# A mixture-of-experts stage: nested branches, fixed sets of blocks, other chunk sizes

## The chip, the cores and the metric

The kernel runs on one core of a Trainium2 chip. The metric is the device time of one launch in microseconds, lower is better. The engines are named as in the profile: PE (TensorE: matmuls; PEld is its weight load), DVE (VectorE), ACT (ScalarE), POOL (GpSimd) and SP (SyncE, here only a queue for DMAs).

## The reference, cut to what matters

Two layers on x of shape 32 x 128 x 56 x 56 in fp32. The first is a depthwise 7x7 convolution, a LayerNorm over the channels and a mixture of 8 experts; the second is a coordinate attention with a 3x3 convolution.

```python
T = N * H * W                                  # 100352 tokens of C = 128
logits = xf @ Wg + bg
topv, topi = jax.lax.top_k(logits, 2)          # two experts for each token
wts = softmax(topv)
order = argsort(-wts[:, 0])                    # the surest tokens first
cap = int(1.25 * T / 8)                        # 15680 places for each expert
# a token beyond its expert's places gets nothing from that expert
h = gelu(eb @ W1[e] + b1[e])                   # 128 -> 512
y = h @ W2[e] + b2[e]                          # 512 -> 128
moe[token] = sum over its experts of gate * y
x = input + x_skip + layer_scale * moe
# second layer
x_h, x_w = means of x over rows and columns    # (and over their first halves and quarters)
a_h, a_w = sigmoid(...), sigmoid(...)
out = conv3x3(x * a_w * a_h); out = out * sigmoid(out)   # with a batch norm between
```

How many tokens an expert gets depends on the data. Here experts 0, 3, 6 and 7 are full (15680), experts 1, 2, 4 and 5 get 7551, 12576, 578 and 1713.

## The kernel before

The stages follow one another: the depthwise convolution (L144, to about 600 us of the profile), LayerNorm, logits and top-2 (L227, to about 1327), the experts (to 3316), and the coordinate attention (L894 to L987, to the end). After the second of these a row for each token lies in DRAM, `acc_d`: its 128 channels, 8 gates and a number of the expert, RW = 137 floats. The change touches only the stage of the experts.

*Blocks and chunks.* An expert's 15680 places are ST = 123 tiles of 128 rows, 4 tiles make a block, so a full expert has 31 blocks. `CHUNKS` cuts the 31 blocks into five chunks. A block passes these steps:

- `gather` (L591): four indirect DMAs, issued by POOL, read 4 x 128 rows of `acc_d` by the list of indices `idx` into a tile `xg`.
- `turn` (L602, L604): PE transposes the four tiles to `pt`, DVE copies them to `fxt`.
- `front` (L612, L613): PE multiplies by W1 into `ph`, ACT applies the gelu and writes `ht`.
- `back` (L621 to L641): PE multiplies by W2 into `py`; DVE computes `own` and the rows to write (`row`, L632, L633), ACT copies the block to `yo` (L636), DVE adds bias, gate and sum (L639 to L641).
- `scatter` (L646): four indirect DMAs, issued by POOL, write the rows of `yo` back to `acc_d` at `row`.

`compute(e, c, ...)` does the middle three for all blocks of a chunk c of expert e, whether they hold tokens or not. `gathers(e, c)` and `scatters(e, c)` are Switches on POOL alone, by the number of blocks that the chunk really holds (`taken_blocks`); a block of a begun chunk without tokens is filled by a memset on POOL (L709) instead of a gather. I write g(e,c) and s(e,c) for these two below.

*Branches.* Around the compute of chunks 1 to 4 stands an If on all engines, `taken > CHUNKS[c] * 512` (L769). The four Ifs of an expert stand behind each other. The next gathers, g(e,c+1), are inside the If; the scatters of the chunk before, s(e,c-1), ahead of it. When the If is not taken, its Else runs only the routing steps that were to be interleaved with the compute.

*Routing.* `Routing` finds by bisection and prefix sums which tokens each expert gets, in small DVE and PE steps. The steps of expert 0 run ahead of the loop; those of the later experts are dealt out over the chunks of the earlier ones (`PIECES`).

*Tiles.* `xg` is a ring of 20 blocks, `yo` and `row` are rings of FO = 16. A block whose slot is in use waits for the reader of the slot. `load_weights` (SP's queue) for expert e+1 stands behind chunk 0 of expert e, `weights` (a multiply of W2 by the layer scale on POOL, L666, and small PE and DVE steps) behind its chunk 1.

*Order.* POOL runs in program order: g(e,1), then for e > 0 the first gathers of the next expert g(e+1,0) (for e = 0 only behind its last chunk), then for each chunk s(e,c-1), If, g(e,c+1), with s(e-1,4) of the expert before at chunk 0. The scheduler that lowers the program moved some of it: for experts 0 to 2 the gathers g(e+1,1) and g(e+2,0) are issued ahead of s(e,3). After the loop a memset on all 16 `yo` slots (the fence) gates the DMAs of the next stage.

## Time and profile before

| | us |
|---|---|
| median of 3 runs | 4523.59 (4507.34 to 4524.99) |
| profiled execution, its own time | 4519.41 |
| its span | 4517.7 |
| stage of the experts in it (1327 to 3316) | 1989 |
| PE, DVE, ACT, POOL busy in that stage | 1502, 984, 698, 1404 |
| granted TensorE clock, whole span | 0.888 |

In the profile's rows "A 4.2 [10.04 <-B]" means that the engine was idle for 10.04 us ahead of the instruction and that B is what the records put as the last thing to release it; "issue" stands for no wait that is seen. Branches, semaphore instructions and the issue of DMAs by a queue do not count as busy, so a stretch of control flow looks like an idle engine. Where both are written, the two numbers of a group's row after the count are the busy time in us and the mean of one in ns.

### The profile page before, as it was taken

The numbers are of one execution on the slowest core, as the hardware profiler recorded it, in microseconds if no ns is written. First come the engines' busy times: TensorE is split into PE (matmuls) and PEld (weight loads), VectorE is DVE, ScalarE is ACT, GpSimd is POOL, SyncE is SP. The second block draws the span as 40 slices with busy tenths as digits, with TensorE's granted clock in tenths as the row PEclk, the third lists the DMA queues.
The fourth block names the chain that finished last, engine by engine and source line by source line (L and its number), as shares of the span: only waits on it lengthen the run. The fifth ranks groups of instructions, "written<-read, shape, count | busy, mean of one in ns | idle before, by whom it ended". The sixth has DMA issues, their size and how long they took to land. (4 is left out here: it accounts for less than half of the span.)

```text
span 4517.7 us, 59987 instructions
## 1 busy us (share of the span) xinstructions
PE 3625.3 (80%) x21360; PEld 2369.6 (52%) x21360; DVE 2569.1 (57%) x5914; ACT 1411.3 (31%) x3132; POOL 2550.8 (56%) x1983
## 2 busy tenths in 40 slices
PE   9999998676328896788788446697958999999899
PEld 4555448676316665565565334464634544455444
DVE  1111115888866966886743112232358888888786
ACT  1111115555203432334243222343412333333232
POOL 1000102232217777668677437777769787877775
PEclk9999998787658898798898778898979999999999
DMA  9999995545362121111111111111155555555552
GB/s 172 217 230 216 230 192 195 231 183 236 150 230 56 49 59 51 44 44 46 52 52 56 46 34 52 56 56 56 56 164 187 174 191 194 168 190 171 176 161 77
DMA packets 814971, 587.33 MB, mean 130 GB/s; under 512 B 545984, under 2 KB 751312, under 8 KB 802128
## 3 DMA queue, kind: packets, MB, share of 16 engines
q1 hardware_dynamic: 508816, 328.72, 25.3%
q10 hardware_dynamic: 262336, 157.84, 12.4%
q0 software_dynamic: 43264, 94.64, 7.3%
q8 instruction: 193, 3.16, 0.3%
q14 instruction: 362, 2.97, 0.2%
HBM read 320.96 MB, written 260.09 MB: 129 GB/s over the span
## 5 line engine op out<-in xcount | busy, mean ns | idle before, releaser
L591 POOL DMA_INDIRECT xg<-acc_d,idx x676 | 673.1, 996 | 408.7 <-issue 172.5
L646 POOL DMA_INDIRECT acc_d<-yo,row x676 | 717.1, 1061 | 234.8 <-issue 82.8
L612 PE MATMUL ph<-fxt,w 128*128 128x512 f32 (+1 forms) x1440 | 700.8, 631 | 53.7 <-ACT ht L613 53.7
L613 ACT ACTIVATE ht<-ph,bias 128x512 f32<-128x512 f32 (+1 forms) x720 | 489.5, 682 | 703.7 <-PE ph L612 702.6
L977 PE MATMUL pc<-v,wk 128*128 128x392 f32 x1920 | 706.1, 510 | 0.4 <-POOL v L962 0.4
L621 PEld LDWEIGHTS py<-w,ht 128*128 128x128 f32 x5728 | 664.9, 192 | 64.8 <-issue 58.2
L621 PE MATMUL py<-w,ht 128*128 128x128 f32 x5728 | 670.5, 276 | 0.0
L144 PE MATMUL acc<-xt,band 56*64 56x424 f32 (+3 forms) x7168 | 666.5, 528 | 2.7 <-POOL band L132 2.7
L144 PEld LDWEIGHTS acc<-xt,band 56*64 56x64 f32 x7168 | 337.6, 133 | 331.0 <-issue 273.3
L977 PEld LDWEIGHTS pc<-v,wk 128*128 128x128 f32 x1920 | 349.2, 192 | 308.6 <-issue 105.7
L227 PE MATMUL lnps<-proj,lnyt 128*128 128x136 f32 x1568 | 354.7, 400 | 138.8 <-ACT sq L232 71.8
L612 PEld LDWEIGHTS ph<-fxt,w 128*128 128x128 f32 x1440 | 279.5, 206 | 329.0 <-issue 243.1
L636 ACT ACTIVATE yo<-xg,own 128x137 f32<-128x137 f32 x716 | 238.0, 401 | 634.9 <-DVE own L632 369.6
L227 PEld LDWEIGHTS lnps<-proj,lnyt 128*128 128x128 f32 x1568 | 349.4, 319 | 144.6 <-ACT sq L232 74.5
L157 DVE TENSOR_SCALAR yt<-acc,dwb 128x448 f32<-128x448 f32 x128 | 87.5, 684 | 582.2 <-PE acc L144 425.2
L639 DVE TENSOR_TENSOR ys<-py,b 128x512 f32<-128x512 f32 (+2 forms) x184 | 123.8, 675 | 490.8 <-PE py L621 480.8
L602 PE MATMUL pt<-ident,xg 128*128 128x128 f32 x716 | 137.0, 311 | 329.7 <-issue 159.2
L132 POOL COPY band<-hk 56x392 f32<-56x392 f32 x128 | 65.2, 510 | 572.4 <-issue 502.0
L987 DVE SCALAR_TENSOR_TENSOR y<-pc,y 128x392 f32<-128x392 f32 x640 | 317.6, 554 | 17.7 <-PE pc L977 17.6
L957 POOL TENSOR_TENSOR d<-pad 128x3248 f32<-128x3248 f32 x32 | 228.1, 7127 | 171.2 <-DVE pad L949 171.2
L894 POOL TENSOR_TENSOR cxn<-cxn,cx 128x896 f32<-128x896 f32 x112 | 261.5, 2344 | 68.3 <-DMA cxn<-acc_d 24.5
L602 PEld LDWEIGHTS pt<-ident,xg 128*128 128x128 f32 x716 | 96.3, 161 | 357.9 <-issue 311.2
(225 smaller groups left out, 4653.8 us busy)
## 6 DMA issues: line engine op xcount, KB each, us to landing
xt<-in_x SPq DMA_DIRECT2D x128, 392.0 KB
y_d<-yt ACTq DMA_DIRECT2D x256, 196.0 KB
lnyt<-y_d SPq DMA_DIRECT2D x16, 3136.0 KB
x<-in_x SPq DMA_DIRECT2D x16, 3136.0 KB
cxn<-acc_d SPq DMA_DIRECT2D x112, 448.0 KB
cx<-acc_d SPq DMA_DIRECT2D x112, 448.0 KB
out<-y ACTq DMA_DIRECT2D x64, 784.0 KB
acc_d<-xn SPq DMA_DIRECT2D x16, 1712.5 KB
```

The source lines that it names most:

```text
L144: nc.tensor.matmul(acc[c][half * G : (half + 1) * G, :, lo:hi], lhsT=band[rows, dw, :], rhs=xt[rows, im, lo + s : hi + s], start=(n == 0), ...
L227: nc.tensor.matmul(ps[:, j, :], lhsT=yf[:, self.j0 + g + j, :], rhs=proj, start=True, stop=True)
L591: d = nc.gpsimd.indirect_dma_start(out=xg[0:n, k, :], out_offset=None, in_=acc_d[0:T1, :], in_offset=bass.IndirectOffsetOnAxis(ap=idx[0][0 ...
L602: nc.tensor.transpose(pt[:, k * P : k * P + n], xg[0:n, k, 0:C], ident[0:n, 0:n])
L612: nc.tensor.matmul(ph[:, 0:N_], lhsT=w[0][:, f * P : (f + 1) * P], rhs=xt[:, 0:N_], start=True, stop=True)
L613: nc.scalar.activation(ht[:, f, 0:N_], ph[:, 0:N_], AF.Gelu, bias=w[2][:, f : f + 1])
L621: nc.tensor.matmul(py[0:n, k, :], lhsT=ht[:, f, k * P : k * P + n], rhs=w2[:, f, :], start=(f == 0), stop=(f == NF - 1))
L636: nc.scalar.activation(yo[0:n, k, :], xg[0:n, k, :], AF.Copy, scale=own[0:n, k : k + 1])
L646: d = nc.gpsimd.indirect_dma_start(out=acc_d[:, :], out_offset=bass.IndirectOffsetOnAxis(ap=row[0:n, k : k + 1], axis=0), in_=yo[0:n, k, : ...
L894: nc.gpsimd.tensor_tensor(xn, xn, x2, ALU.add)
L977: nc.tensor.matmul(m[k], lhsT=wk[k][:, dw, :], rhs=v[:, k, rows, dw : dw + W], start=(dw == 0), stop=(dw == 2))
L987: nc.vector.scalar_tensor_tensor(r[x], m[k], f, r[y_], ALU.mult, ALU.add)
```

## The change

The chunks become 4, 7, 7, 7 and 6 blocks (they were 4, 8, 8, 8 and 3). The Ifs of an expert are nested: `chunk(e, c)` calls `chunk(e, c + 1)` inside its own If, so the first one not taken leaves all later chunks, with their Switches, at once; its Else runs all routing steps that are left. The ring of `xg` becomes two sets of 4 blocks for chunk 0, by turns of the expert, and two sets of 7 for the others, by turns of the chunk. `yo` and `row` become two sets of 7, by turns of `e * 5 + c`. The weights of the next expert are loaded and multiplied directly behind compute(e, 0). The first gathers of expert 1 stand behind the whole nest of expert 0.

```diff
@@ -30,9 +30,9 @@
 BLK = 4
 
 
-CHUNKS = (0, 4, 12, 20, 28, -(-ST // BLK))
+CHUNKS = (0, 4, 11, 18, 25, -(-ST // BLK))
 NC_ = len(CHUNKS) - 1
-CB = 8
+CB = 7
 RW = C + E + 1
 T1 = T + P
 ZF = 16
@@ -554,13 +554,12 @@
                 return out
 
 
-        FO = 16
         cp1 = st.enter_context(tc.tile_pool(name="fc", bufs=1))
         wp = st.enter_context(tc.tile_pool(name="fw", bufs=2))
-        xp = st.enter_context(tc.tile_pool(name="fx", bufs=20))
+        xp = st.enter_context(tc.tile_pool(name="fx", bufs=1))
         tp = st.enter_context(tc.tile_pool(name="ft", bufs=2))
         hp = st.enter_context(tc.tile_pool(name="fh", bufs=2))
-        op = st.enter_context(tc.tile_pool(name="fo", bufs=FO))
+        op = st.enter_context(tc.tile_pool(name="fo", bufs=1))
         xsp = st.enter_context(tc.tile_pool(name="fs", bufs=2))
         ptp = st.enter_context(tc.tile_pool(name="fpt", bufs=1, space=PSUM))
         php = st.enter_context(tc.tile_pool(name="fph", bufs=3, space=PSUM))
@@ -575,7 +574,14 @@
                           .rearrange("p x (e c) -> p (x e) c", e=E))
         nc.vector.tensor_tensor(b2, b2, bc(ls_bc.unsqueeze(1), [P, E, C]), ALU.mult)
 
-        zr = op.tile([P, BLK, RW], F32, tag="yo", name="zr2")
+
+
+        xg_first = [[xp.tile([P, BLK, RW], F32, name=f"xg_f{k}_{s}") for s in range(CHUNKS[1])] for k in range(2)]
+        xg_rest = [[xp.tile([P, BLK, RW], F32, name=f"xg_r{k}_{s}") for s in range(CB)] for k in range(2)]
+        yo_all = [[op.tile([P, BLK, RW], F32, name=f"yo_{k}_{s}") for s in range(CB)] for k in range(2)]
+        row_all = [[op.tile([P, BLK], I32, name=f"row_{k}_{s}") for s in range(CB)] for k in range(2)]
+
+        zr = yo_all[1][CB - 1]
         nc.gpsimd.memset(zr, 0.0)
         for k in range(2):
             r0, n = T1 + ZA * T // ZF + k * T // 4, T // 4 // P // BLK
@@ -622,8 +628,9 @@
                                      start=(f == 0), stop=(f == NF - 1))
             nb, t0 = len(blocks[i]), blocks[i][0][0]
             own = sp.tile([P, BLK], F32, tag="own", name=f"own{e}_{i}")
-            row = sp.tile([P, BLK], I32, tag="row", bufs=FO, name=f"row{e}_{i}")
-            yo = op.tile([P, BLK, RW], F32, tag="yo", name=f"yo{e}_{i}")
+            c = max(c for c in range(NC_) if CHUNKS[c] <= i)
+            turn_, k_ = (e * NC_ + c) % 2, i - CHUNKS[c]
+            row, yo = row_all[turn_][k_], yo_all[turn_][k_]
             ys = xsp.tile([P, BLK, C], F32, tag="ys", name=f"ys{e}_{i}")
             whole = [x for x in blocks[i] if x[1] == P]
             parts = [(0, len(whole), P)] if whole else []
@@ -701,8 +708,8 @@
                         others(s)
 
         def rows_for(e, c):
-            for s in chunks[c]:
-                xgs[e, s] = xp.tile([P, BLK, RW], F32, tag="xg", name=f"xg{e}_{s}")
+            for k, s in enumerate(chunks[c]):
+                xgs[e, s] = xg_rest[c % 2][k] if c else xg_first[e % 2][k]
 
         def gathers(e, c, parts):
             taken_blocks(e, c, parts, lambda s: gather(e, s, idxs[e], xgs[e, s]),
@@ -739,6 +746,29 @@
                 skip_runtime_bounds_check_because="it is limited to the blocks of the largest chunk")
             return parts
 
+        def first_of_next(e):
+            if e + 1 < E:
+                parts[e + 1] = counted(e + 1)
+                rows_for(e + 1, 0)
+                gathers(e + 1, 0, parts[e + 1])
+
+        def chunk(e, c, w, steps):
+
+            scatters(e, c - 1, parts[e])
+            if c + 1 < NC_:
+                rows_for(e, c + 1)
+            with tc.If(taken > CHUNKS[c] * BLK * P, preferred_fallthrough_block=True) as some:
+                if c + 1 < NC_:
+                    gathers(e, c + 1, parts[e])
+                compute(e, c, w, steps[c])
+                if c + 1 < NC_:
+                    chunk(e, c + 1, w, steps)
+            left = [f for fs in steps[c:] for f in fs]
+            if left:
+                with some.Else():
+                    for f in left:
+                        f()
+
 
         PIECES = (16, 32, 32, 24, 16), (16, 32, 28, 16, 8)
         for f in some_routing(ready[0]):
@@ -750,43 +780,26 @@
         for e in range(E):
             _, (taken,) = nc.values_load_multi_w_load_instructions(
                 idxs[e][2], min_val=0, max_val=CAP, skip_runtime_bounds_check_because="it counts an expert's tokens")
-            for c in range(NC_):
-
-                if c:
-                    scatters(e, c - 1, parts[e])
-                elif e:
-                    scatters(e - 1, NC_ - 1, parts[e - 1])
-                if c + 1 < NC_:
-                    rows_for(e, c + 1)
-                if c == 0:
-                    gathers(e, 1, parts[e])
-                if c == (0 if e else NC_ - 1) and e + 1 < E:
-                    parts[e + 1] = counted(e + 1)
-                    rows_for(e + 1, 0)
-                    gathers(e + 1, 0, parts[e + 1])
-                steps = some_routing(PIECES[e > 0][c])
-                if c:
-                    with tc.If(taken > CHUNKS[c] * BLK * P, preferred_fallthrough_block=True) as some:
-                        if c + 1 < NC_:
-                            gathers(e, c + 1, parts[e])
-                        compute(e, c, w, steps)
-                    if steps:
-                        with some.Else():
-                            for f in steps:
-                                f()
-                else:
-                    compute(e, c, w, steps)
-                if e + 1 < E:
-                    if c == 0:
-                        w_next = load_weights(e + 1)
-                    if c == 1:
-                        w_next = weights(e + 1, *w_next)
-            w = w_next
+            if e:
+                scatters(e - 1, NC_ - 1, parts[e - 1])
+            rows_for(e, 1)
+            gathers(e, 1, parts[e])
+            if e:
+                first_of_next(e)
+            steps = [some_routing(n) for n in PIECES[e > 0]]
+            compute(e, 0, w, steps[0])
+            if e + 1 < E:
+                w = weights(e + 1, *load_weights(e + 1)), w
+            else:
+                w = None, w
+            chunk(e, 1, w[1], steps)
+            if e == 0:
+                first_of_next(0)
+            w = w[0]
         scatters(E - 1, NC_ - 1, parts[E - 1])
 
         fence = []
-        for k in range(FO):
-            yo = op.tile([P, BLK, RW], F32, tag="yo", name=f"yo_end{k}")
+        for yo in yo_all[0] + yo_all[1]:
             fence.append(nc.vector.memset(yo[:, :, 0:1], 0.0).ins)
     pr_stack.close()
 
```

## Prediction

> **What bounds the kernel now.** I read the busy shares first, then the slices, then one window for each stage.

> ```profile
> span 4517.7 us, 59987 instructions
> PE 3625.3 (80%) x21360; PEld 2369.6 (52%) x21360; DVE 2569.1 (57%) x5914; ACT 1411.3 (31%) x3132; POOL 2550.8 (56%) x1983
> ...
> L591 POOL DMA_INDIRECT xg<-acc_d,idx x676 | 673.1, 996 | 408.7 <-issue 172.5
> L646 POOL DMA_INDIRECT acc_d<-yo,row x676 | 717.1, 1061 | 234.8 <-issue 82.8
> ```

> By busy shares TensorE leads. But the diff touches only the expert stage, 1327 to 3316 us. The windows answer for that stage, and for its last part (experts 6 and 7), reads:

> ```profile
> 1327.00:3316.00 1989.00, 1502.02 (x8426) 1094.71 (x8426) 983.84 (x2543) 697.79 (x1436) 1403.72 (x1374) 0.86 0.18 51
> 2769.00:3315.80 546.80, 423.99 (x2406) 309.68 (x2405) 162.09 (x345) 203.48 (x414) 416.28 (x429) 0.89 0.19 57
> ```

> The columns are PE, PEld, DVE, ACT, POOL. In the second row POOL issues 428 indirect DMAs and one multiply in 546.8 us, 1.28 us per DMA, and its timeline has no hole: each row follows with the 0.30 us of "issue" that stands between any two. A gather (0.94 busy) has a pitch of 1.25, a scatter (0.97) of 1.275. So 1352 DMAs x 1.26 = about 1706 of the 1989 us are POOL's queue of DMAs, and nothing else sets the pace of a full expert: 123 gathers and 123 scatters are 311 us, while TensorE needs 31 blocks x 7.45 us = 231 us (period from the timeline: ph at 2597.91, next at 2605.36).

> What is not DMA pitch is holes in POOL's timeline. The large ones:

> ```profile
> 1861.05 0.95 POOL L646 DMA_INDIRECT acc_d<-yo,row  x1 [10.04 <-ACT yo L636]
> ...
> 1884.92 0.98 POOL L591 DMA_INDIRECT xg<-acc_d,idx  x1 [8.18 <-DVE thr_r L420]
> ```

> ```profile
> 2170.95 0.97 POOL L591 DMA_INDIRECT xg<-acc_d,idx  x1 [9.35 <-DVE mid_r L421]
> ```

> ```profile
> 2616.05 0.97 POOL L591 DMA_INDIRECT xg<-acc_d,idx  x1 [49.00 <-PE ph L612]
> ```

> ```profile
> 2643.27 1.26 POOL L666 TENSOR_TENSOR w<-w,ls_bc 128x512 f32<-128x512 f32 x1 [7.12 <-PEq L769]
> 2648.32 1.01 POOL L646 DMA_INDIRECT acc_d<-yo,row  x1 [3.80 <-issue]
> 2698.49 0.97 POOL L591 DMA_INDIRECT xg<-acc_d,idx  x1 [30.19 <-DVE ys L639]
> 2765.11 1.54 POOL L666 TENSOR_TENSOR w<-w,ls_bc 128x512 f32<-128x512 f32 x1 [6.17 <-PE ph L612]
> 2768.95 1.01 POOL L646 DMA_INDIRECT acc_d<-yo,row  x1 [2.30 <-issue]
> ```

> The releasers in brackets were done long before. What the holes share is control flow: at 1861 a Switch with a part of zero DMAs, at 1884 a branch not taken, at 2170 a zero Switch, and in the 49.00 and 30.19 us experts 4 and 5. Those hold 578 and 1713 tokens (2 and 4 blocks); chunks 1 to 4 are not taken, and each leaves one If and one zero Switch. The sequencer records of 2569 to 2604 show three such pairs in 35 us: 11.6 us a pair, a branch of about 3 us and bumps of the DMA semaphores of 2.3 us on either side. All holes over 0.45 us sum to 173 us. Outside these places the sequencer runs some 8 DMAs (10 us) ahead, so a taken If or a full Switch is hidden.

> **The change part by part.** Blocks needed per expert, from the DMAs seen: 31, 15, 25, 31, 2, 4, 31, 31.

> *Chunk bounds.* Blocks computed go from 31+20+28+31+4+4+31+31 = 180 to 31+18+25+31+4+4+31+31 = 175. That is 5 x 7.45 = 37 us of TensorE, worth nothing on the path: POOL's 311 us per full expert cover TensorE's 231, and the DMAs stay at 676 + 676. If POOL were not the bound, they would be worth 37. The memsets that fill missing blocks are one per block, 10 to 5: 5 x 0.57 = -2.8 on POOL. Expert 2 needs exactly 25 blocks, now the end of a chunk: one partial Switch with its drain goes. From 2170 on, 105.2 us held 60 DMAs; 72 at the mean pitch with the drains left would take 111.7, and the 12 more DMAs at 1.275 would be 15.3: -8.7. Expert 1 (15 blocks) loses one zero Switch, but a drain moves to the partial gather of a later chunk: +2. A first chunk of expert 0 followed by 7 blocks and not 8 starts the scatters 4 gathers sooner, but blocks 2 and 3 are then the late ones: +3.

> *Nesting.* For experts 4 and 5 one branch not taken replaces four, and the Switches of chunks 2 to 4 are jumped over. From the end of s(3,3) (2508.5) to the first scatter of expert 6 (2769.0) are 260.5 us with 115 DMAs: 115 x 1.26 = 145, so 115 of holes (10.4 + 4.9 + 49.0 + 7.1 + 3.8 + 30.2 + 6.2 + 2.3 = 113.9). I lay the new program order on it, 0 being the end of s(3,3): zero Switch g(4,1) 9.5; 23 scatters s(3,4) to 38.8; weights multiply to 40.4; 16 gathers g(6,0) to 60.4; 8 scatters s(4,0) to 73.5; If not taken, zero Switches g(5,1) and s(4,4), multiply, 24.5 in all, to 98; g(7,0), paced by the compute of expert 5, to 122; s(5,0) to 143; If not taken to 150; 28 gathers g(6,1) to 185; zero Switch s(5,4) and multiply to 195. These are 107 DMAs (135 us) and 60 us of holes: 115.5 - 60 = -55. The 8 DMAs that left this stretch stand elsewhere and cancel.

> [...] The trace shows 11.6 us for an If and a zero Switch. [...] I go by the row: two holes of 49 and 30 us stand exactly where the pairs are. [...] TensorE's far jumps in this stretch took 3.6 to 4.6 us each; if a longer one costs the same, one replaces four.

> *The leaving of a nest.* A full expert now ends with four exits in a row. Before, they lay between chunks. Four bumps and jumps at 2.3 to 5 us are 9 to 20 us, of which the 10 us lead hides most; bounds 0 and +10 for each of the experts 0, 3, 6 and 7. I take 0, as the eight taken Ifs of experts 6 and 7 cost nothing visible now, and keep +40 for the range.

> *Fixed sets of xg.* g(1,0) waited 5.64 us (at 1608) for a slot of the ring of 20; it now has a set of its own and stands later: -5.6. Elsewhere the block it overwrites was read before the scatters ahead of it on POOL.

> *Fixed sets of yo and row, 14 instead of 16.* The first chunk of an expert now writes the set of s(e,3), which stands behind g(e,4). From the end of s(e,3), POOL has g(e+1,1) 35, s(e,4) 29, multiply and g(e+2,0) 21: 85 us until s(e+1,0). The compute of 4 blocks is there after about 50 to 56. Slack 30; before expert 7, without a g(8,0), 8. No cost; if the cover is gone, a late block stalls POOL one for one.

> *Order.* g(e+1,1) and g(e+2,0), which stood ahead of s(e,3) for the first experts, stand behind it now; the same DMAs on one queue. The weights are loaded and multiplied earlier; SP's loads landed about 3 us after issue, and a multiply is 1.37 us. A late load holds the multiply, and behind it POOL's next gathers: 3 us at most each. 0. The Else branches run all remaining routing steps at once; VectorE has the same steps, and while it runs the bit steps POOL's DMAs stretch to as much as 5.2 us (84 us in sum). This is moved, not removed: 0, bounds -20 and +20.

> Sum: -2.8 - 8.7 + 2 + 3 - 55 - 5.6 = -67. The convolution stage that follows (1201 us, TensorE 1081 busy) only starts sooner. Against the profiled execution (4519.4; span 4517.7 and 1.7 around it) this gives 4452. It lies 4 us under the median 4523.6, so I say 4455.

> **The rivals.**

> *A. Half of the control stays.* Else branches of nested Ifs must settle the semaphores of all levels, so a jump over four levels may cost two or three pairs. For it: bumps of 2.3 us stand on both sides of each branch already. Against: the number of bumps follows the lanes, not the levels. The gain of nesting then falls from 55 to 15 or 35: 4475 to 4500.

> *B. TensorE is the bound, or nothing is.* The page's chain is mostly PE; then 5 blocks fewer give -37, 4482. If the holes are waits for data, as their releasers say, almost nothing: 4505 to 4530. Against both: experts 6 and 7 without a hole on POOL, TensorE busy 424 of 547.

> *C. Slower: a taken nested If drains the DMA lanes, as the zero Switch does now.* There are 21 taken Ifs after the change (4, 2, 3, 4, 0, 0, 4, 4). At the 8 us of the drain at 1884 that is +168 against -67: about 4620. It decides from (67 + 22.6)/21 = 4.3 us per taken If. Against: a taken If in experts 6 and 7 costs nothing now, and its inside is the same. For: exits in a row, and the lead of 10 us is used up once by them.

> *D. The branch is not entered as said*, for instance all chunks still visited: 4515 to 4525. The nested call inside the If makes this unlikely.

> **How the numbers follow.** My forecast (4425 to 4475) 0.56; A 0.16; B with 37 us 0.05; B without gain, or D, or exits that eat the gain 0.10; C or late yo blocks 0.13. A measurement of this kernel can tell about 0.5%, 22.6 us: faster is below 4501, slower above 4546. Faster 0.77, same 0.10, slower 0.13. The range reaches from my forecast with the stretch of routing at its good end (4425) over A and B up to the gainless cases' middle, 4520; outside lie C, the upper half of the gainless ones, and little below.

> **What would show it.** Right: POOL's holes of 49.00 and 30.19 us become one near 25 and one near 7; s(3,3) to the first scatter of expert 6 takes about 195 us; 1352 indirect DMAs at the same 1.25 and 1.275 pitch; 5 memsets; pt x696; the convolution stage as long as before. Wrong: holes of 8 us or more at taken Ifs of experts 0, 3, 6 and 7 (C), a hole ahead of the first scatters of expert 7 with "ACT yo" as releaser (yo sets), or the holes of experts 4 and 5 still there (A, B).

## The result: 1% faster, and the profile after

The changed kernel takes 4471.12 us (median of 6 runs, 4459.04 to 4488.94) against 4513.04 for the kernel before (6 runs, 4502.84 to 4524.99). The ratio is 0.990, 95% interval 0.9877 to 0.9922. A second measurement beside the experiments gave 0.9885 (0.9866 to 0.9905). So the gain is 42 us by the first pair of medians and 48 by the second; the sum of the prediction was 67, and 4471 lies near the upper end of its own forecast, 4425 to 4475. The profiled execution took 4459.04 us, the lowest of its six, so its profile shows the gain somewhat too large. One session of the experiments, that of the near and the far jumps, was about 12% slower for every kernel in it (5067.17 us for the kernel before), so its two kernels are compared with each other alone.

The page of the kernel after; after the bar stand the busy time in us and the mean of one in ns:

```profile
span 4457.0 us, 59552 instructions
PE 3584.7 (80%) x21140; PEld 2320.7 (52%) x21140; DVE 2550.8 (57%) x5882; ACT 1393.5 (31%) x3092; POOL 2550.7 (57%) x1978
...
L653 POOL DMA_INDIRECT acc_d<-yo,row x676 | 695.9, 1029 | 249.3 <-issue 75.1
...
L597 POOL DMA_INDIRECT xg_r<-acc_d,idx x556 | 579.5, 1042 | 178.7 <-issue 114.6
```

POOL does the same work as before: 2550.7 us busy against 2550.8, five instructions (memsets) fewer. PE loses 40 us of work over the whole span. The windows of the stage of the experts, of experts 6 and 7 in it, and of the stage that follows (columns PE, PEld, DVE, ACT, POOL):

```profile
1331.00:3259.00 1928.00, 1465.70 (x8206) 1065.77 (x8206) 966.21 (x2511) 680.02 (x1396) 1399.16 (x1359) 0.86 0.19 53
3259.00:4457.00 1198.00, 1075.75 (x4112) 566.14 (x4112) 971.17 (x1382) 361.37 (x350) 928.86 (x384) 0.96 0.53 172
```

```profile
2710.80:3264.50 553.70, 448.65 (x2521) 325.08 (x2520) 168.54 (x354) 218.71 (x448) 422.25 (x433) 0.90 0.20 57
```

Experts 6 and 7 issue 432 DMAs in 553.7 us, 1.28 us each as before (428 in 546.8). Here POOL's timeline again has no hole, with eight taken Ifs, now nested, inside this window. The holes that are left at experts 4 and 5, from POOL's timeline:

```profile
2525.65 0.95 POOL L653 DMA_INDIRECT acc_d<-yo,row  x1 [9.87 <-DVE ys L647]
...
2608.33 1.27 POOL L673 TENSOR_TENSOR w<-w,ls_bc 128x512 f32<-128x512 f32 x1 [15.43 <-PE ph L618]
2615.17 1.00 POOL L597 DMA_INDIRECT xg_f<-acc_d,idx  x1 [5.57 <-DVE yo L648]
...
2622.08 0.94 POOL L597 DMA_INDIRECT xg_f<-acc_d,idx  x1 [2.14 <-DVE yo L648]
...
2629.09 0.94 POOL L597 DMA_INDIRECT xg_f<-acc_d,idx  x1 [2.32 <-DVE yo L648]
...
2665.61 0.98 POOL L597 DMA_INDIRECT xg_r<-acc_d,idx  x1 [6.01 <-DVE row L640]
...
2706.96 1.26 POOL L673 TENSOR_TENSOR w<-w,ls_bc 128x512 f32<-128x512 f32 x1 [6.01 <-PE pt L608]
2710.87 1.01 POOL L653 DMA_INDIRECT acc_d<-yo,row  x1 [2.65 <-ACT ht L619]
```

The 49.00 us became 15.43 + 5.57, the 30.19 us became 6.01. s(3,3) ends at 2515.78, s(6,0) begins at 2710.87: 195.1 us for 107 DMAs.

A sum over the timeline shows where the time went. I cut the stage at the first scatter of each expert; a hole is an idle time of POOL over 0.45 us, and the stretch is what the DMAs took beyond 0.955 us each. The hole ahead of a cut counts to the row above it.

| from | us before | us after | DMAs | holes before, after | stretch before, after |
|---|---|---|---|---|---|
| first gather | 60.7 | 55.3 | 48, 44 | 0, 0 | 0, 0 |
| s(0,0) | 358.5 | 374.7 | 262, 262 | 5.6, 3.5 | 21.9, 40.5 |
| s(1,0) | 216.5 | 232.4 | 120, 128 | 34.9, 47.2 | 27.5, 23.6 |
| s(2,0) | 304.2 | 291.9 | 192, 200 | 25.5, 18.1 | 34.6, 21.1 |
| s(3,0) | 287.4 | 291.3 | 214, 218 | 10.4, 9.9 | 6.5, 5.9 |
| s(4,0) | 94.2 | 62.6 | 24, 24 | 64.5, 33.6 | 0.3, 0.2 |
| s(5,0) | 120.6 | 71.2 | 64, 44 | 38.7, 14.7 | 0.4, 0.5 |
| s(6,0) | 293.2 | 295.3 | 230, 230 | 0, 0 | 3.5, 5.6 |
| s(7,0) | 253.6 | 258.3 | 198, 202 | 0.7, 0 | 4.1, 4.1 |
| all | 1988.9 | 1932.9 | 1352, 1352 | 180.3, 127.0 | 99.0, 101.4 |

The stage is 56 us shorter, and the holes are 53 us fewer. In the second profile of the changed kernel the stage took 1941.1 us, so about 8 us lie within the scatter from run to run. Ahead of the stage the profile of after is 4.6 us later and behind it 9.3 us shorter. I put these down to scatter: the part behind the stage took 1190 to 1205 us across all profiles.

### The profile page after: what moved, and what is told of

Same layout as the page of the kernel before. It is cut to its first block, busy times and chain, and to the rows that moved or that the text cites. A ratio compares the mean times of both kernels' runs of the same rounds, so it can differ in the third digit from the quotient of the medians.

```text
span 4457.0 us, 59552 instructions
## 1 busy us (share of the span) xinstructions
PE 3584.7 (80%) x21140; PEld 2320.7 (52%) x21140; DVE 2550.8 (57%) x5882; ACT 1393.5 (31%) x3092; POOL 2550.7 (57%) x1978
## 5 line engine op out<-in xcount | busy, mean ns | idle before, releaser
L653 POOL DMA_INDIRECT acc_d<-yo,row x676 | 695.9, 1029 | 249.3 <-issue 75.1
L597 POOL DMA_INDIRECT xg_r<-acc_d,idx x556 | 579.5, 1042 | 178.7 <-issue 114.6
L627 PEld LDWEIGHTS py<-w,ht 128*128 128x128 f32 (+1 forms) x5568 | 644.8, 192 | 62.8 <-issue 56.2
L618 PE MATMUL ph<-fxt,w 128*128 128x512 f32 (+1 forms) x1400 | 677.0, 627 | 0.0
L627 PE MATMUL py<-w,ht 128*128 128x128 f32 (+1 forms) x5568 | 650.6, 275 | 0.0
L144 PEld LDWEIGHTS acc<-xt,band 56*64 56x64 f32 x7168 | 321.2, 133 | 351.5 <-issue 284.0
L646 DVE TENSOR_TENSOR ys<-py,b 128x512 f32<-128x512 f32 (+1 forms) x179 | 120.2, 673 | 482.7 <-PE py L627 479.8
L643 ACT ACTIVATE yo<-xg_r,own 128x137 f32<-128x137 f32 (+1 forms) x568 | 191.4, 402 | 393.3 <-DVE own L639 296.0
L907 POOL TENSOR_TENSOR cxn<-cxn,cx 128x896 f32<-128x896 f32 x112 | 260.5, 2333 | 73.7 <-DMA cxn<-acc_d 36.8
L608 PE MATMUL pt<-ident,xg_r 128*128 128x128 f32 (+1 forms) x568 | 116.4, 317 | 231.4 <-DMA xg_r<-acc_d,idx 162.5
L250 DVE SCALAR_TENSOR_TENSOR xn<-cen,rstd,gamma_bc 128x128 f32<-128x128 f32 x784 | 219.5, 339 | 100.8 <-POOL rstd L241 100.8
```

The source lines that it names most:

```text
L144: nc.tensor.matmul(acc[c][half * G : (half + 1) * G, :, lo:hi], lhsT=band[rows, dw, :], rhs=xt[rows, im, lo + s : hi + s], start=(n == 0), ...
L250: nc.vector.scalar_tensor_tensor(xn[:, j, :], self.cen[:, j, 0:C], rstd[:, j : j + 1], gamma_bc, ALU.mult, ALU.mult)
L597: d = nc.gpsimd.indirect_dma_start(out=xg[0:n, k, :], out_offset=None, in_=acc_d[0:T1, :], in_offset=bass.IndirectOffsetOnAxis(ap=idx[0][0 ...
L618: nc.tensor.matmul(ph[:, 0:N_], lhsT=w[0][:, f * P : (f + 1) * P], rhs=xt[:, 0:N_], start=True, stop=True)
L627: nc.tensor.matmul(py[0:n, k, :], lhsT=ht[:, f, k * P : k * P + n], rhs=w2[:, f, :], start=(f == 0), stop=(f == NF - 1))
L653: d = nc.gpsimd.indirect_dma_start(out=acc_d[:, :], out_offset=bass.IndirectOffsetOnAxis(ap=row[0:n, k : k + 1], axis=0), in_=yo[0:n, k, : ...
```

## The experiments

My theory: POOL's queue is the bound, and nesting removes control flow of experts 4 and 5 from it. Rivals: the fixed sets, the earlier weights or the order bring the gain; or TensorE's 5 blocks do.

**All Ifs flat again.**

```diff
                     gathers(e, c + 1, parts[e])
                 compute(e, c, w, steps[c])
-                if c + 1 < NC_:
-                    chunk(e, c + 1, w, steps)
-            left = [f for fs in steps[c:] for f in fs]
-            if left:
+            if steps[c]:
                 with some.Else():
-                    for f in left:
+                    for f in steps[c]:
                         f()
+            if c + 1 < NC_:
+                chunk(e, c + 1, w, steps)
```

> The changed kernel with its Ifs laid flat again, as before; chunk sizes, fixed sets, the earlier weights and the place of g(1,0) as changed. If the gain is the control flow of experts 4 and 5 (my theory), the two long holes of POOL come back, s(3,3) to the first scatter of expert 6 takes 245 to 255 us instead of 195, and the time is 0 to 15 us under the kernel before (ratio 0.997 to 1.000). If the gain comes from the fixed sets, the earlier weights or the 5 blocks less, it stays: 40 to 60 us under it (0.987 to 0.991), the stretch at about 195.

Measured: 4577.46 us, ratio 1.0136 (1.0118 to 1.0153). Both expectations missed it: it is not level with the kernel before but 62 us slower, 111 slower than the changed kernel. The stretch from s(3,3) to s(6,0) took 239.1 us, 44 more than nested, a little short of the forecast. The rest is elsewhere: 24 us more holes from s(1,0) on, 16 from s(2,0) on, and 21 us at the very end. The first two were not looked into. DVE's timeline of this kernel shows what that last one is:

```profile
3270.61 0.06 DVE L802 MEMSET yo<- 128x4 f32 x1 [43.65 <-DMA acc_d<-yo,row]
3270.87 0.43 DVE L639 TENSOR_SCALAR own<-xg_r 128x4 f32<-128x4 f32 x2 [0.20 <-issue]
```

L802 is the fence that belongs behind the last scatter. It was scheduled ahead of compute(7,3), and that compute waited for s(7,2) behind it. So this kernel is no clean undoing of the nest, and a narrower one was needed.

**Flat for experts 4 and 5 alone.** The same edit, under `flat = e in (4, 5)`.

> The changed kernel with the nest undone for experts 4 and 5 alone (their Ifs stand behind each other as before). My sum gave nesting 55 us there; the kernel with all Ifs flat showed 44 us more of holes between s(3,3) and s(6,0). Theory: that stretch goes from 195 to 240 to 250 us, and the time is 40 to 55 us over the changed kernel, ratio to before 0.998 to 1.002. Rival (the nest pays mostly at experts 1 and 2, and flat Ifs hurt through waits on the fixed sets elsewhere): less than 25 us over the changed kernel, ratio under 0.995.

Measured: 4524.17 us, ratio 1.0021 (1.0005 to 1.0036), against 4466.55 and 0.9885 of the changed kernel. POOL's timeline:

```profile
2631.61 1.27 POOL L673 TENSOR_TENSOR w<-w,ls_bc 128x512 f32<-128x512 f32 x1 [38.13 <-PE pt L608]
2641.54 0.99 POOL L597 DMA_INDIRECT xg_f<-acc_d,idx  x1 [8.66 <-DVE yo L648]
...
2710.64 0.98 POOL L597 DMA_INDIRECT xg_r<-acc_d,idx  x1 [24.43 <-issue]
...
2758.43 1.27 POOL L673 TENSOR_TENSOR w<-w,ls_bc 128x512 f32<-128x512 f32 x1 [13.07 <-PE ph L618]
2767.96 1.01 POOL L653 DMA_INDIRECT acc_d<-yo,row  x1 [8.26 <-ACT ht L619]
```

From s(3,3) to s(6,0) it needs 252.0 us, a little over the forecast of 240 to 250, and the changed kernel 195.1. All of it lies from s(4,0) to s(6,0): 190.5 us against 133.8 in both profiles of the changed kernel. Those 57 us are the whole difference of the two kernels (57.6 by the medians, which come from two sessions whose kernels before agree within 1.4 us). The rest of the change, with this nest undone, is not faster than the kernel before. That shows where the gain comes from; the rival falls.

**Chunk bounds alone**, in the kernel before: `CHUNKS = (0, 4, 11, 18, 25, 31)`, `CB = 7`.

> The kernel before with only the chunk bounds changed to 4, 7, 7, 7, 6 (rings of 20 and 16 kept, flat Ifs): 175 blocks computed instead of 180. Theory (POOL is the bound): 5 memsets and one drain less, 5 to 12 us faster (ratio 0.997 to 0.999). Rival (TensorE is the bound): 5 x 7.45 = 37 us faster (0.992).

Measured: 4520.69 us, ratio 1.0006 (0.9994 to 1.0018). No gain, neither the 37 us of the rival nor my 5 to 12. The window of the stage (the columns as above), with PE's and POOL's busy time:

```profile
1329.00:3326.00 1997.00, 1477.95 (x8206) 1075.47 (x8206) 967.00 (x2510) 677.68 (x1396) 1413.42 (x1365) 0.85 0.19 51
```

PE works 24 us less than before there (1502.02), and the stage is no shorter. From s(0,0) to s(1,0) it takes 375.0 us against 358.5, with 40.0 us of stretch against 21.9. So the 18 us of stretch that the changed kernel shows at expert 0 come with the bounds alone. From s(2,0) to s(3,0) it takes 288.3 us instead of 304.2, with 10 us less of stretch and 5.5 less of holes, so most of it comes back there. Why the stretch moves was not found: VectorE's routing steps took 202 us at expert 0 before and 201 with these bounds.

**What a pair of If and Switch is made of.** A zero Switch is one whose chunk holds no blocks. Two kernels add three zero Switches or three Ifs to the Else of chunk 1, which only experts 4 and 5 run.

```diff
                 with some.Else():
                     ...
+                    if c == 1:
+                        for k in (2, 3, 4):
+                            rows_for(e, k)
+                            gathers(e, k, parts[e])            # three_switches
+                            with tc.If(taken > CHUNKS[k] * BLK * P, ...):   # or: three_ifs
+                                compute(e, k, w, [])
```

> The changed kernel with three Switches g(e,2), g(e,3), g(e,4) added in the Else of chunk 1, so that experts 4 and 5 pass three zero Switches each, without an If. If a zero Switch costs about half of the 11.6 us of a pair: 6 x 4 to 6 = 24 to 36 us over the changed kernel. If the price of a pair is that of the If: under 10 us.

> The changed kernel with three Ifs on all engines (taken > bound of chunks 2, 3, 4; their body is the compute of that chunk) added in the Else of chunk 1, so that experts 4 and 5 pass three Ifs not taken each, without a Switch. If an If costs about half of a pair: 6 x 5 to 7 = 30 to 42 us over the changed kernel. If the Switches carry the price, or the jumps of TensorE are hidden behind POOL: under 12 us.

Measured: the Switches 4491.83 us, ratio 0.9949 (0.993 to 0.9968); the Ifs 4468.85 us, ratio 0.9904 (0.9879 to 0.9928). POOL's timeline of the first, then of the second:

```profile
2631.71 1.26 POOL L673 TENSOR_TENSOR w<-w,ls_bc 128x512 f32<-128x512 f32 x1 [33.43 <-issue]
...
2708.53 0.98 POOL L597 DMA_INDIRECT xg_r<-acc_d,idx  x1 [28.14 <-PE ph L618]
```

```profile
2602.51 1.27 POOL L673 TENSOR_TENSOR w<-w,ls_bc 128x512 f32<-128x512 f32 x1 [16.25 <-PE ph L618]
...
2660.38 0.98 POOL L597 DMA_INDIRECT xg_r<-acc_d,idx  x1 [6.25 <-DVE row L640]
```

Three zero Switches lengthen the hole of expert 4 from 15.43 to 33.43, 6.0 us each. At expert 5 the hole goes from 6.01 to 28.14, but there the sequencer's records show four zero Switches ahead of g(6,1) and not three, about 5.5 us each: s(5,4), which stood behind g(6,1) in the changed kernel, stands ahead of it here. From s(4,0) to s(6,0) this kernel needs 161.3 us, 27.5 more than the changed one, within the 24 to 36 that were expected if a Switch is half of a pair. Three Ifs lengthen the two holes by 0.8 and 0.2 us in all. But POOL had nothing to jump over in these Ifs. The sequencer's records (start in us, and what came next) tell the kinds apart. EVENT_SEMAPHORE is where the branch has landed; INC_SWDGE_SEM is the bump of the DMA semaphores (the lanes) that follows:

```
three_ifs   2590.81 COMPARE_BRANCH   2590.97 COMPARE_BRANCH   2591.13 COMPARE_BRANCH   2591.30 next
flat_45     2594.46 COMPARE_BRANCH (If)             2597.71 EVENT_SEMAPHORE      3.25 us
            2598.14 INC_SWDGE_SEM                   0.37 us
            2598.72 COMPARE_BRANCH (into Switch)    2599.85 BRANCH_PREFETCH_HINT 1.13 us
            2600.65 COMPARE_BRANCH (out of Switch)  2603.12 COMPARE_BRANCH (If)  2.47 us
            2603.12 to 2611.57, one whole pair                                   8.45 us
            2625.82 COMPARE_BRANCH (If of chunk 4)      2625.99 next            0.17 us
after       2594.57 COMPARE_BRANCH (If, past all four chunks)   2597.23 EVENT_SEMAPHORE   2.66 us
            2597.65 INC_SWDGE_SEM                   0.37 us
```

The If of chunk 4 in the kernel with flat Ifs has no gathers inside, so POOL passes it, in 0.17 us, as it passes the three empty ones in 0.16 to 0.17.

**Near and far.** To separate the length of the jump from the settling of the DMA lanes, the body of the three Ifs was given work of POOL: a whole Switch g(e,k), or one block's 4 gathers.

```diff
                             with tc.If(taken > CHUNKS[k] * BLK * P, ...):
+                                gathers(e, k, parts[e])                                       # ifs_far
+                                gather(e, chunks[k][0], idxs[e], xgs[e, chunks[k][0]])        # or: ifs_near
                                 compute(e, k, w, [])
```

> As three_ifs (three Ifs not taken in the Else of chunk 1), but the body of each also holds a Switch g(e,k) on POOL, so that POOL has to jump over some 150 to 400 instructions for each. In the kernel with experts 4 and 5 flat, such a jump took 3.0 to 3.25 us on POOL; in three_ifs, with nothing of POOL in the body, 0.16 us. Theory (the price is the distance of the jump): 6 x 3.0 = 18 us, with the settling of lanes up to 25 us over the changed kernel. Rival (the price is that of the Switches and the lanes they settle): under 6 us.

> As three_ifs, with a body in which POOL has one block's 4 gathers, so that POOL jumps over some ten instructions. The lanes of these DMAs must be settled behind each If, as for a Switch. Theory (distance): under 6 us over the changed kernel, the hole in expert 4 at 15 to 18 us. Rival (settling the lanes is what costs, wherever the jump goes): 10 to 25 us, like the far one.

Measured: far 5001.43 us, ratio 0.9882 (0.9846 to 0.9918); near 4987.59 us, ratio 0.9844 (0.9812 to 0.9877). The changed kernel was not run beside them, so the forecasts over it can't be tested, and the two intervals overlap; the traces decide. From s(4,0) to s(6,0) the far one needs 152.6 us, the near one 139.3. The six branches took 3.30, 2.47, 2.49, 3.29, 2.50 and 2.66 us in the far one, and 2.15, 0.18, 0.18, 0.18, 0.18 and 0.17 in the near one. That is 16.7 against 3.0 us in all, which accounts for the 13 us between them. Behind each If both wait for the lanes, the far one for eight and the near one for four, and the bump takes as long in the two (0.34 to 0.37 and 0.36 to 0.38 us at expert 4). So the price goes with what stands to be jumped over, a whole Switch or four gathers. Beyond a Switch it did not grow: 2.66 us past four chunks, 3.25 past one. Why the first near branch took 2.15 us is open.

**s(e,4) inside the innermost If.**

```diff
                 compute(e, c, w, steps[c])
                 if c + 1 < NC_:
                     chunk(e, c + 1, w, steps)
+                else:
+                    scatters(e, c, parts[e])
...
-            if e:
-                scatters(e - 1, NC_ - 1, parts[e - 1])
...
-        scatters(E - 1, NC_ - 1, parts[E - 1])
```

> The changed kernel with s(e,4) moved into the innermost If, so that an expert whose last chunk is not taken meets no zero Switch for it (experts 1, 2, 4, 5). Theory (a zero Switch costs 6 to 10 us wherever it stands): 20 to 30 us faster than the changed kernel, ratio to before 0.983 to 0.986. Rival (the scatters now stand right behind s(e,3), before compute(e,4) is done, and g(e+1,1) comes 29 us later): POOL waits 10 us or more at each of the full experts, the gain is eaten, 0.989 to 0.993, with holes ahead of s(0,4), s(3,4), s(6,4), s(7,4).

Measured: 4449.00 us, ratio 0.9835 (0.9817 to 0.9853): the fastest of all, 17.6 us under the changed kernel on the same chip, and the two intervals do not overlap. The forecast of 20 to 30 us was a little high. From s(1,0) to s(2,0) it needs 223.0 us and not 232.4 (holes 34.5 instead of 47.2); no new holes stand at the full experts. Expert 5 gave 7 us (64.4 instead of 71.2). Expert 4 gave nothing, and its timeline says why:

```profile
2595.24 1.27 POOL L673 TENSOR_TENSOR w<-w,ls_bc 128x512 f32<-128x512 f32 x1 [12.51 <-PE ph L618]
2606.38 1.00 POOL L597 DMA_INDIRECT xg_f<-acc_d,idx  x1 [9.87 <-DVE yo L648]
```

Without the zero Switch the multiply comes after 12.51 us instead of 15.43. The next gathers g(7,0) then wait 9.87 instead of 5.57, until compute(5,0) has let go of the block that they overwrite. A hole of control has turned into a wait for data.

**g(e,1) inside the If of chunk 1 as well**: in the kernel just told, `gathers(e, 1, ...)` moved to the head of that If.

> The kernel with s(e,4) in the innermost If, and g(e,1) moved into the If of chunk 1, right ahead of g(e,2); so experts 4 and 5 meet no zero Switch g(e,1) either. Theory (a zero Switch costs 7 to 10 us): holes of 9 and 10 to 15 us ahead of s(3,4) and in expert 4 go, 12 to 20 us faster than with s(e,4) alone, ratio to before 0.979 to 0.981. Rival (s(e,0) now stands before g(e,1), with no 35 us of gathers between, and waits for compute(e,0)): holes of 5 to 15 us ahead of s(3,0), s(6,0), s(7,0), no gain or slower, 0.983 to 0.990.

Measured: 4581.69 us, ratio 1.0156 (1.0134 to 1.0179). The rival was right, and by more than it said. POOL's timeline at the start of the stage:

```profile
1383.76 1.01 POOL L653 DMA_INDIRECT acc_d<-yo,row  x1 [34.80 <-ACT ht L619]
...
1390.68 0.97 POOL L653 DMA_INDIRECT acc_d<-yo,row  x1 [2.06 <-ACT ht L619]
...
1397.76 0.96 POOL L653 DMA_INDIRECT acc_d<-yo,row  x1 [2.29 <-issue]
```

g(0,1), which took 35 us, was what POOL did while compute(0,0) ran. Now POOL stands still for 34.80 us. At the start of expert 6 it stands still for 17.11 us; ahead of s(3,0) and s(7,0), where the rival expected holes too, there is none and one of 2.02. The largest loss was in nobody's forecast: the holes between s(1,0) and s(2,0) are 96.7 us instead of the 34.5 of the kernel just told, and those up to s(3,0) 37.7 instead of 17.8. What these wait for was not looked into.

## Why the prediction was right, point by point

- **POOL is the bound.** Shown: five blocks fewer, 24 us less of PE in the stage, brought nothing with the bounds alone (1.0006), and experts 6 and 7 run at 1.28 us per DMA in both kernels. The first half of rival B falls.
- **The nest at experts 4 and 5, -55.** The laid-out stretch came to 195 us; both profiles have 195.1. The time beyond 1.26 us for each DMA goes from 115.6 to 60.3. The pacing of g(7,0) by compute(5,0) is in the timeline (2.14 and 2.32). Undoing this part alone costs 57 us. Rival B's other half (the holes are waits for data) falls for the long holes; the 5.57 us and the pacing are waits for data.
- **The price of a pair.** 11.6 us were read for the kernel before, at expert 4; at its expert 5 a pair takes 9.2, and with experts 4 and 5 flat in the changed kernel one takes 8.45. The bumps differ: two of 2.3 us in a pair at expert 4 before, two of 0.9 at expert 5, two of 0.37 in the flat kernel, and why is not shown. It was right to go by the row: in the kernel before the sequencer's 37 semaphore waits inside the 49.00 us sum to 1.3 us, and its 31 inside the 30.19 us to 1.1. A branch not taken into its body took 0.17 to 0.18 us where that body held four gathers (one took 2.15) and 2.47 to 3.30 where it held a Switch. What a far branch does in that time no run here shows; that the time goes with what it jumps over the near and far kernels show.
- **Rival A**, half of the control stays: no. The one jump past all four chunks took 2.66 us at expert 4 and 2.87 at expert 5, one past a single chunk 3.25, and behind the one of 2.66 stand waits for eight lanes, as in the kernel before behind a jump past one chunk, and a single bump of 0.37 us. The 3.6 to 4.6 us read for TensorE's far jumps were 2.3 to 5.3 us by its sequencer's records; the sum did not use them.
- **Rival C**, a taken nested If drains the lanes: no. There are no holes from s(6,0) to the end. With them the exits of the nest, kept as up to 40, are 0.
- **The yo sets and the slack of 8 us ahead of s(7,0):** no hole there. The ring of xg and the first chunk: predicted -5.6 and +3, the holes of expert 0 went from 5.6 to 3.5.
- **The stretch, moved and not removed:** 99.0 before, 101.4 after. It moved from experts 1 and 2 to expert 0, which the bounds alone do too.
- **Where the sum was mis-sized: experts 1 and 2.** The steps were "+2" and "-8.7", together -6.7. The holes from s(1,0) to s(3,0) went from 60.4 to 65.3, +4.9. The term is 11.6 us off, which is about the difference between the forecast -67 and the -56 of the stage. At expert 2 the number came near, -7.4, but for another reason. No drain of its own Switches went: behind the partial g(2,3) the kernel before shows no hole, and the zero Switch g(2,4) still costs 8.73 us at 2179 (9.35 before), since 25 full blocks leave chunk 4 empty as they did before. What went is the partial g(4,0), which had 7.1 us of holes behind it at 2227 to 2239. It moved to expert 1, where the holes grew by 12.3 us and not by 2:

```profile
1970.31 0.99 POOL L597 DMA_INDIRECT xg_f<-acc_d,idx  x1 [4.08 <-PE ps_r L408]
1972.33 0.95 POOL L597 DMA_INDIRECT xg_f<-acc_d,idx  x1 [1.03 <-DMA xg_r<-acc_d,idx]
1974.31 0.94 POOL L597 DMA_INDIRECT xg_f<-acc_d,idx  x1 [1.03 <-ACT yo L643]
...
1987.14 0.94 POOL L597 DMA_INDIRECT xg_f<-acc_d,idx  x1 [3.69 <-ACT yo L643]
...
1993.89 1.26 POOL L653 DMA_INDIRECT acc_d<-yo,row  x1 [4.75 <-issue]
```

The first seven of the 8 DMAs of this case went out every 2.0 us, with a bump of 1.4 to 1.5 us ahead of each on the sequencer, and left holes of 3.69 and 4.75 us. In the kernel before, g(4,0) stood behind the 32 DMAs of g(3,1), so the sequencer was ahead (its first bump for them at 2206.95, the first of the 8 at 2211.38, the bumps 0.9 to 1.0 us each) and the 8 went at 1.25. I had counted the end of the case only, not the loss of that lead.

- **One reading:** all holes over 0.45 us in the kernel before sum to 180 us, not to 173. The forecast does not rest on it.

## What to carry to other kernels

In these traces POOL's control flow shows as idle time put down to a releaser that did not hold it (49.00 us "<-PE ph", of which 1.3 us are the sequencer's semaphore waits); read the sequencer's records there before taking it for a wait for data. What cost time here is a jump over much code (2.47 to 3.32 us each, against 0.17 to 0.18 over four gathers): put code that is seldom run behind one branch, and order nested cases so that one jump skips them all. But before a step is moved into a branch, look at what it covers: the 35 us of gathers, moved so that two short experts skip a Switch, had been the cover of compute(0,0).
